# Attention in two passes over 16 head groups: the second pass starts 9 units behind the first, not 12

## The chip, the cores and the metric

The kernel runs on one core of one Trainium2 chip. The metric is the device time of one execution in microseconds. The kernel before took 2340.22 us, the median of three runs (2337.09 to 2341.55). The engines are named as the profile names them: PE is TensorE (matmuls and transposes), DVE is VectorE, ACT is ScalarE, POOL is GpSimd, and SP issues most of the DMAs. PSUM is the memory that PE writes its results to; a tile of it must be read out by DVE or ACT before PE can write there again.

## The reference

The input is four sequences of 1024 tokens with 256 features. The program is a layer stack: attention, a mixture of experts (4 experts, one per token), a Mamba2 block and the mixture again, each added to its input after a layernorm. The change lies in attention alone, which is, cut to what matters:

```python
ids = _adapter_ids(lora_start_indices, b)            # one low-rank adapter per sequence
Q = _multilora(x, ids, Wq, Aq, Bq)                   # K and V in the same way
Q, K, V = (split(Q), split(K), split(V))             # 16 heads of 16 features
Q, K = (_rope(Q), _rope(K))
scores = jnp.einsum('bhqd,bhkd->bhqk', Q, K) / jnp.sqrt(jnp.asarray(D_KV, x.dtype))
causal = jnp.tril(jnp.ones((s, s), bool))
scores = jnp.where(causal, scores, jnp.asarray(-jnp.inf, scores.dtype))
attn = jax.nn.softmax(scores, axis=-1)
out = jnp.einsum('bhqk,bhkd->bhqd', attn, V)
return _multilora(out, ids, Wo, Ao, Bo)
```

The softmax needs the maximum of each query's scores before the exponentials, and this is why the kernel computes the scores twice.

## The kernel before

**Groups and passes.** Attention treats 16 groups one after the other (`Heads`, numbered n): four sequences, and in each four groups of four heads. A group goes through three kinds of work.

- *Pieces* prepare its operands (`piece`, L833). `rotated` multiplies 256 tokens with the merged weights (qkv, L780), applies the rotary embedding on POOL, and `split` divides each query and key into a rounded value and a remainder, so that matmuls with rounded operands keep the precision. `turn` (L824) transposes 512 tokens of them with four PE transposes, and ACT casts the result to SBUF (L831).
- *The first pass* is 12 units (`first_pass`, L951): query block qb of 128 queries against keys 0 to 511 (h = 0) or 512 to 1023 (h = 1), as far as the causal mask allows. In `maxima` (from L848) each unit has two halves p of two heads: two score matmuls (L857) into a PSUM tile of two banks, a mask addition on DVE where the block touches the diagonal (L865), and a maximum on DVE (L866). The widths of the units in order are 128, 256, 384, 512, 512, 128, 512, 256, 512, 384, 512, 512; units 0, 1, 2, 3, 5, 7, 9 and 11 have the mask. `negated` (L868 to L885) turns the maxima of 512 queries around: a few small DVE operations into the tile mm, four PE transposes into a PSUM tile (L883), and a DVE copy to mneg (L885). It runs for queries 0 to 511 after unit 3 and for queries 512 to 1023 after the last unit.
- *The second pass* is also 12 units (`second_pass`, L952): query half qt of 512 queries against key block kc of 128 keys. Units 0 to 3 have qt = 0 with widths 512, 384, 256 and 128; units 4 to 11 have qt = 1 with 512 five times and then 384, 256, 128. Each half p recomputes the scores with keys on the partitions (L893), adds the negated maxima by a second pair of matmuls with mneg, takes the exponential on ACT (L901), and cuts the diagonal block on POOL (L904). `weigh` (L912) then multiplies with the values, in four column tiles of 32, into one accumulator bank, and `divide` sends the sums out and back to divide them. Units from 4 on need the mneg of the second half of the queries.

**Order.** `attention` is written as loops. In a prologue before the second pass of group 0, the list `beside` puts pieces of group 0 and group 1 next to the 12 first-pass units of group 0. Then the loop over n goes through the 12 units u of group n's second pass. Beside unit u stands unit u of the first pass of group n + 1 (through `look`), a piece of group n + 2, and steps of generators: `begin` starts the next sequence's layernorm and transposes, `finish` multiplies with the output weights and routes tokens to experts, and `tiles` are tiles of the first mixture of experts. `weigh` of a unit runs in the unit behind it. The two last turns of a group, those for tokens 512 to 1023 (pieces 12 and 13), come at units 0 and 1 of the next group's loop. A scheduler takes this program and sets the order of each engine's queue by its own plan, so that the queues differ from the written order where data allow it.

**PSUM.** In attention, PSUM is cut into three tiles of two banks for the scores of both passes (and for the experts), one tile of a single bank, and one bank for the accumulator. The single bank serves, one after another in program order, the turns, qkv, mneg, the transposes of the layernorm's output (xT), the output projection and the routing. In the prologue, turns and qkv use the two-bank tiles instead.

Of the kernel before, what the change touches and what calls it, by code (L numbers as in the profile page):

```python
# [78 lines left out]
def hybrid_block(ctx: ExitStack, tc: tile.TileContext, t, out: bass.AP):  # L79
# [81 lines left out]
    def layernorm(pool, xs, xln, name, pinned=False):  # L161
        n = xs.shape[1]
        stats = pool.tile([P, n, 6], F32, tag="ln_stats", name=f"stats_{name}", bufs=2)
        mv = pool.tile([P, n, 2], F32, tag="ln_mv", name=f"mv_{name}", bufs=2)
        rstd = pool.tile([P, n], F32, tag="ln_rstd", name=f"rstd_{name}", bufs=2)
        for i in range(n):
            first = nc.vector.bn_stats(stats[:, i, :], xs[:, i, :])
            if pinned and i == 0:
                tc.keep_in_program_order(first)
            nc.vector.bn_aggr(mv[:, i, :], stats[:, i, :])  # L170
        nc.vector.tensor_single_scalar(rstd, mv[:, :, 1], EPS, op=ALU.add)
        rsqrt(rstd, name)
        shift = pool.tile([P, n], F32, tag="ln_shift", name=f"shift_{name}", bufs=2)
        nc.vector.scalar_tensor_tensor(shift, mv[:, :, 0], -1.0, rstd, op0=ALU.mult, op1=ALU.mult)
        for i in range(n):
            nc.scalar.activation(
                xln[:, i, :], xs[:, i, :], AF.Identity, bias=shift[:, i : i + 1], scale=rstd[:, i : i + 1]
            )

    def transposed(xln, dst, name):  # L180

        for k in range(2):
            pt = ps1(f"xT_{name}_{k}")
            for i in range(4):
                nc.tensor.transpose(pt[:, i * P : (i + 1) * P], xln[:, i, k * P : (k + 1) * P], ident)
            evacuate(k, dst[:, k, :], pt)
# [430 lines left out]
    def attention(pa):  # L617
# [54 lines left out]
        def merge(b, weff):  # L672
            btm = pa.tile([LR, HG, 3, 64], F32, tag="btm", name=f"btm_{b}")
            nc.vector.tensor_scalar_mul(btm, bt_qkv, msk[:, b : b + 1])
            for k in range(2):
                pm = ps2(f"merge_{b}_{k}")
                for h in range(2):
                    for w in range(3):
                        nc.tensor.matmul(
                            pm[:, h, 0:384].rearrange("p (c w e) -> p c w e", c=2, w=3)[:, :, w, :],  # L680
                            a_qkv[:, w, k * P : (k + 1) * P],
                            btm[:, 2 * h : 2 * h + 2, w, :],
                            start=True,
                            stop=True,
                        )
                nc.vector.tensor_tensor(
                    weff[:, k, :].rearrange("p (h o) -> p h o", h=2),
                    pm[:, :, 0:384],
                    weff[:, k, :].rearrange("p (h o) -> p h o", h=2),
                    ALU.add,  # L690
                )
            return weff
# [16 lines left out]
        def begin(b):  # L709
            B = batches[b] = Batch()  # L710
            B.xT = pa.tile([P, 2, SEQ], F32, tag="xT", name=f"xT_{b}")
            B.o = [pa.tile([P, SEQ], F32, tag="o", name=f"o_{b}_{k}", bufs=3) for k in range(2)]
            for g in range(2):
                other = b == 0 and g == 1
                xln = pa.tile([P, 4, D], F32, tag="pe" if other else "x", name=f"x_{b}_{g}", bufs=4 if other else 1)
                nc.sync.dma_start(xln, t["x"][b, g * TB : (g + 1) * TB].rearrange("(n p) d -> p n d", p=P))
                if g == 0:
                    weff = pa.tile([P, 2, HG * 192], F32, tag="weff", name=f"weff_{b}")
                    nc.sync.dma_start(weff, t["w_qkv"].rearrange("(k p) o -> p k o", p=P))
                if b == 0:  # L720
                    yield
                layernorm(pa, xln, xln, f"a{b}_{g}")
                if g == 0:
                    B.weff = merge(b, weff)
                yield
                transposed(xln, B.xT[:, :, g * 512 : (g + 1) * 512], f"a{b}_{g}")
                yield
# [223 lines left out]
        first_pass = [(qb, h) for qb in range(NBLK) for h in range(qb // 4 + 1)]  # L951
# [3 lines left out]
        def look(H, u, p):  # L955
            qb, h = first_pass[u]
            H.maxima(qb, h, p)
            if p == 0:
                return
            if (qb, h) == (3, 0):  # L960
                H.negated(0)
            if u == len(first_pass) - 1:
                H.negated(1)


        first = begin(0)
        next(first)
        load_more()
# [3 lines left out]
        H, after = heads[0], heads[1]  # L972
# [4 lines left out]
        for which in range(2):  # L977
# [9 lines left out]
            lambda: after.project(2),  # L987
            lambda: [after.turn(0, 1, p) for p in range(2)],
            lambda: after.project(3),
            lambda: [after.turn(1, 0, p) for p in range(2)],  # L990
            lambda: [after.turn(1, 1, p) for p in range(2)],
            lambda: None,
        ]
        for u in range(len(first_pass)):
            beside[u]()
            for p in range(2):
                look(H, u, p)
# [29 lines left out]
        for n, H in enumerate(heads):  # L1027
            after = heads[n + 1] if n + 1 < len(heads) else None
            then = heads[n + 2] if n + 2 < len(heads) else None
            for u, (qt, kc) in enumerate(second_pass):  # L1030
                if after and n and u < 2:
                    after.piece(12 + u)

                pes = []
                for p in range(2):
                    off, pe = H.exps(qt, kc, p)
                    pes.append(pe)
                    if after:
                        look(after, u, p)
                    if p == 0:  # L1040
                        weigh_late()
                late = (H, qt, kc, off, pes)
                step()
                if then:
                    then.piece(u)
                if H.c == 0 and n and u == 6:
                    sending = finish(H.b - 1, 1)
                if H.c == HG - 1 and u == 10:
                    sending = finish(H.b, 0)
                if H.c == 1 and H.b + 1 < NB and u == 8:  # L1050
                    starting = begin(H.b + 1)
                next(starting, None)
                next(sending, None)
                if u not in (0, 1, 5, 6):
                    next(tiles, None)
                if H.c == 1 and n > 1 and u == 1:
                    for _ in tiles:
                        pass
                    tiles = stage(2 * H.b)
# [382 lines left out]
    for n, H in enumerate(halves):  # L1442
        after = halves[n + 1] if n + 1 < len(halves) else None
# [94 lines left out]
```

## Time and profile before

| what | value |
|---|---|
| median of three runs | 2340.22 us |
| the profiled execution | 2337.63 us |
| its span, first to last instruction | 2335.9 us |
| mean granted PE clock | 0.946 |
| PE busy in the span | 2121.0 us, 91% |
| DVE busy | 1375.6 us, 59% |
| ACT busy | 866.6 us, 37% |
| POOL busy | 844.7 us, 36% |
| maxima of the first pass on DVE (L866), 384 | 363.7 us |
| exponentials on ACT (L901), 384 | 308.8 us |
| weigh matmuls on PE (L912), 1536 | 263.5 us |
| first matmul of the second pass of group 0 | at 82.6 us |
| last matmul of the second pass of group 15 | at 1160.1 us |

The span is one execution. Busy time is a sum over an engine's instructions, with overlap counted once. The shares are averages over the whole program; the stage that the change touches is the first half. The clock is the share of full speed that the chip granted to PE.

### The profile page before, as it was taken

The page shows a single profiled execution, that of the slowest core. Times are in us where ns is not written, and L with a number is a line of the kernel's source. Part 1 is how long each engine was busy: PE and PEld are TensorE (multiplying, and loading weights), DVE is VectorE, ACT ScalarE, POOL GpSimd, SP SyncE. Part 2 cuts the span into 40 slices and gives each one's busy share as a digit, 9 for nine tenths or more (in the row PEclk, how much of TensorE's full clock was granted, in tenths as well). Part 3 has the DMA queues.
Part 4 walks back from the last instruction along what each step waited for, and adds up shares of the span by engine and source line. Part 5 has one row for each costly group of instructions (what it writes and reads, how often), then busy time and mean ns, then how long its engine had stood idle before and what let it go on. Part 6 is the DMA issues. An engine that isn't in the chain of part 4 may idle for free. (4 is left out here: it accounts for less than half of the span.)

```text
span 2335.9 us, 34795 instructions
## 1 busy us (share of the span) xinstructions
PE 2121.0 (91%) x12322; PEld 1484.7 (64%) x12322; DVE 1375.6 (59%) x3536; ACT 866.6 (37%) x1709; POOL 844.7 (36%) x1455
## 2 busy tenths in 40 slices
PE   5899998999999998999988986989899999999997
PEld 4444454554455555655677983557677777879887
DVE  5666666656655455655254336777777777676422
ACT  3365544455544443343310114444333333332110
POOL 3343434244443333321111213665535343343121
PEclk8799998999999999999999997899999999899999
DMA  9101011300132121132246780002435354344788
GB/s 332 33 28 42 22 35 56 104 24 20 44 127 84 59 83 60 41 126 81 95 153 231 252 284 27 1 28 70 159 109 192 108 188 147 131 160 149 272 301 305
DMA packets 148976, 278.19 MB, mean 119 GB/s; under 512 B 19964, under 2 KB 92030, under 8 KB 148800
## 3 DMA queue, kind: packets, MB, share of 16 engines
q1 hardware_dynamic: 120768, 227.98, 28.3%
q0 software_dynamic: 9920, 30.25, 3.5%
q10 hardware_dynamic: 18112, 17.70, 2.5%
q8 instruction: 100, 1.64, 0.3%
q14 instruction: 76, 0.62, 0.1%
HBM read 225.17 MB, written 51.12 MB: 118 GB/s over the span
## 5 line engine op out<-in xcount | busy, mean ns | idle before, releaser
L866 DVE TENSOR_REDUCE mx<-s 128x2 f32<-128x1024 f32 (+3 forms) x384 | 363.7, 953 | 82.8 <-PE s L857 76.6
L901 ACT ACTIVATE pe<-s 128x1024 f32<-128x1024 f32 (+3 forms) x384 | 308.8, 810 | 247.2 <-PE s L893 185.2
L912 PE MATMUL acc<-pe,v 128*32 128x512 f32 (+3 forms) x1536 | 263.5, 516 | 13.6 <-POOL pe L904 11.7
L904 POOL TENSOR_SCALAR_AFFINE_SELECT pe<-pe 128x256 f32<-128x256 f32 x256 | 103.9, 407 | 440.4 <-ACT pe L901 440.1
L469 PE MATMUL gu_f<-t_xT_f,t_Wg_f 128*128 128x128 f32 (+1 forms) x1216 | 239.8, 320 | 4.6 <-DVE t_xT_f L141 2.3
L469 PE MATMUL gu_f<-t_xT_f,t_Wu_f 128*128 128x128 f32 (+1 forms) x1216 | 235.3, 317 | 1.6 <-DMA t_Wu_f<-in_Wu 1.6
L469 PEld LDWEIGHTS gu_f<-t_xT_f,t_Wg_f 128*128 128x128 f32 x1216 | 186.8, 196 | 26.9 <-issue 7.1
L865 DVE TENSOR_TENSOR s<-s,amats 128x256 f32<-128x256 f32 x256 | 109.1, 428 | 153.9 <-PE s L857 113.8
L469 PEld LDWEIGHTS gu_f<-t_xT_f,t_Wu_f 128*128 128x128 f32 x1216 | 188.9, 196 | 13.3 <-DMA t_Wu_f<-in_Wu 2.4
L485 PE MATMUL y_f<-t_Wd_f,t_h_f 128*128 128x256 f32 x816 | 187.3, 383 | 7.4 <-DVE t_rows_f L492 2.7
L857 PE MATMUL s<-ks,qs 64*128 64x512 f32 (+3 forms) x768 | 171.8, 398 | 23.1 <-ACT pe L901 13.5
L893 PE MATMUL s<-qs,ks 64*128 64x512 f32 (+3 forms) x768 | 181.7, 439 | 10.1 <-DVE mx L866 7.6
L893 PEld LDWEIGHTS s<-qs,ks 64*128 64x128 f32 x768 | 79.5, 188 | 170.9 <-issue 96.3
L159 DVE SCALAR_TENSOR_TENSOR t_h_f<-t_h_f,gu_f 128x512 f32<-128x512 f32 x102 | 69.8, 684 | 195.5 <-ACT t_h_f L158 195.5
L485 PEld LDWEIGHTS y_f<-t_Wd_f,t_h_f 128*128 128x128 f32 x816 | 152.8, 191 | 38.0 <-issue 6.7
L158 ACT ACTIVATE t_h_f<-gu_f 128x512 f32<-128x512 f32 x102 | 60.8, 596 | 279.1 <-PE gu_f L469 279.1
L893 PE MATMUL s<-mneg,sel_r 64*128 64x512 f32 (+3 forms) x768 | 160.2, 364 | 0.0
L857 PEld LDWEIGHTS s<-ks,qs 64*128 64x128 f32 x768 | 84.3, 194 | 73.9 <-ACT pe L901 26.3
L1221 DVE SCALAR_TENSOR_TENSOR xc_m<-raw_m,conv_w,xc_m 128x512 f32<-128x512 f32 x144 | 112.3, 790 | 22.2 <-ACT xc_m L1217 15.8
L1171 POOL TENSOR_TENSOR m_m<-m_m,gm_m 128x256 f32<-128x256 f32 x128 | 94.2, 768 | 58.1 <-ACT gm_m L1314 57.0
L780 PE MATMUL qkv<-weff,xT 128*128 128x192 f32 x512 | 105.9, 352 | 8.2 <-ACT ks L831 4.6
L780 PEld LDWEIGHTS qkv<-weff,xT 128*128 128x128 f32 x512 | 86.2, 199 | 28.7 <-ACT ks L831 10.5
(448 smaller groups left out, 3935.0 us busy)
## 6 DMA issues: line engine op xcount, KB each, us to landing
t_Wg_f<-in_Wg SPq DMA_DIRECT2D x38, 1024.0 KB
t_Wu_f<-in_Wu SPq DMA_DIRECT2D x38, 1024.0 KB
t_Wd_f<-in_Wd SPq DMA_DIRECT2D x38, 1024.0 KB
sorted_rows<-blank SPq DMA_DIRECT2D x8, 2056.0 KB
t_Wg_f2p<-in_Wg SPq DMA_DIRECT2D x10, 1024.0 KB
t_Wu_f2p<-in_Wu SPq DMA_DIRECT2D x10, 1024.0 KB
t_Wd_f2p<-in_Wd SPq DMA_DIRECT2D x10, 1024.0 KB
t_Wg_f1p<-in_Wg SPq DMA_DIRECT2D x9, 1024.0 KB
```

The costliest lines, as they stand in the source:

```text
L469: nc.tensor.matmul(gu[:, i, j, :], w[which][:, k, f * P : (f + 1) * P], xT[:, k, :], start=(k == 0), stop=(k == 1))
L485: nc.tensor.matmul(y, hs[f // nf][:, f % nf, i * P : (i + 1) * P], wd[:, f, :], start=(f == 0), stop=(f == DFF // P - 1),)
L780: nc.tensor.matmul(pp[:, i, 0:192], B.xT[:, k, tok], B.weff[:, k, self.c * 192 : (self.c + 1) * 192], start=(k == 0), stop=(k == 1),)
L857: nc.tensor.matmul(sc[:, a, 0:w], self.q[p, qb // 4][r, qb % 4 * P : (qb % 4 + 1) * P], self.k[p, h][r, 0:w], start=True, stop=True,)
L865: nc.vector.tensor_tensor(sc[:, :, w - P : w], sc[:, :, w - P : w], bcast(amats, 1, 2), ALU.add)
L866: nc.vector.tensor_reduce(self.mx[:, qb, 2 * p : 2 * p + 2, h], sc[:, :, 0:w], axis=AX.X, op=ALU.max)
L893: nc.tensor.matmul(sc[:, a, off:512], sels[p][r, :] if part else self.k[p, kc // 4][r, kc % 4 * P : (kc % 4 + 1) * P], self.mneg[qt][r, of ...
L901: nc.scalar.activation(pe[:, :, off:512], sc[:, :, off:512], AF.Exp, scale=1.0 / math.sqrt(DK))
L904: nc.gpsimd.affine_select(diag, diag, [[0, 2], [1, P]], ALU.is_ge, 0.0, base=0, channel_multiplier=-1)
L912: nc.tensor.matmul(self.acc[32 * j : 32 * j + 32, off:512], self.v[:, kc, (DK + 1) * j : (DK + 1) * j + 32], pes[j // 2][:, j % 2, off:512 ...
L1171: nc.gpsimd.tensor_tensor(*operands(slice(i, i + size)), op)
L1221: nc.vector.scalar_tensor_tensor(acc, raw[:, k : k + TB], conv_w[:, cc, k : k + 1], acc, op0=ALU.mult, op1=ALU.add)
```

## The change

`LAG` is 9. The prologue computes only the first 9 first-pass units of group 0, and the three last entries of `beside` go: two of them were the four turns of group 1's tokens 512 to 1023, and the last was empty. These turns are now pieces 12 and 13 of the loop for group 0 too. In the loop, unit u of a group's second pass has beside it, for u = 0 to 2, the group's own first-pass units 9 to 11, and for u = 3 to 11 the first-pass units 0 to 8 of the next group. With this, `negated` for the first half of the queries falls at u = 6 of the group before (it was u = 3), and for the second half at u = 2 of the group itself (it was u = 11 of the group before). The last group, which had no first-pass unit beside it, now has its own three.

```diff
+        LAG = 9
+
         first = begin(0)
...
             lambda: after.project(3),
-            lambda: [after.turn(1, 0, p) for p in range(2)],
-            lambda: [after.turn(1, 1, p) for p in range(2)],
-            lambda: None,
         ]
-        for u in range(len(first_pass)):
+        for u in range(LAG):
             beside[u]()
             for p in range(2):
                 look(H, u, p)
...
             for u, (qt, kc) in enumerate(second_pass):
-                if after and n and u < 2:
+                if after and u < 2:
                     after.piece(12 + u)
 
                 pes = []
                 for p in range(2):
                     off, pe = H.exps(qt, kc, p)
                     pes.append(pe)
-                    if after:
-                        look(after, u, p)
+                    ahead = LAG + u
+                    if ahead < len(first_pass):
+                        look(H, ahead, p)
+                    elif after:
+                        look(after, ahead - len(first_pass), p)
                     if p == 0:
                         weigh_late()
```

The functions that are called (`piece`, `turn`, `maxima`, `negated`, `exps`, `weigh`) are the same in both kernels.

## Prediction

> **What bounds the kernel now.** I read first the slices of the span, to see which engine is full where the change acts (attention fills the first half, slices 1 to 20 of 58.4 us each).
>
> ```profile
> PE   5899998999999998999988986989899999999997
> ...
> DVE  5666666656655455655254336777777777676422
> ...
> PEclk8799998999999999999999997899999999899999
> ```
>
> TensorE is 90% busy or more from the third slice on, VectorE 50 to 60%. The exceptions are the first two slices. The table of busy time by stretches splits them (each row: stretch and length in us; then busy time of PE, its weight loads, DVE, ACT, POOL; granted clock; DMA share; GB/s):
>
> ```profile
> core 0: us, PE busy (x) PEld busy (x) DVE busy (x) ACT busy (x) POOL busy (x), PEclk, DMA share, GB/s
> ...
> 60.00:70.00 10.00, 7.37 (x38) 5.55 (x38) 5.74 (x10) 2.41 (x9) 4.08 (x8) 0.84 0.30 94
> 70.00:82.60 12.60, 9.68 (x34) 4.75 (x34) 7.37 (x10) 3.67 (x10) 4.09 (x8) 0.50 0.00 1
> 82.60:137.20 54.60, 51.56 (x290) 25.23 (x290) 36.96 (x76) 28.67 (x57) 22.25 (x47) 0.84 0.03 11
> 137.20:193.00 55.80, 51.70 (x346) 27.55 (x344) 35.28 (x59) 30.23 (x59) 23.98 (x49) 1.00 0.13 44
> ```
>
> 82.6 us is where the second pass of group 0 starts, 137.2 where that of group 1 starts (first L893 matmul of each). Before 82.6 no engine is full and the clock ends at half; from 82.6 on TensorE is busy 92 to 99% of every group. The loop over groups is bound by TensorE, and runs to the last L893 at 1160.1.
>
> The waits of TensorE between 82.6 and 1160.1, longest first, show what is left there:
>
> ```profile
> PE s L857 <- ACT pe L901: 13.5, 17, 1.8
> PE acc L912 <- POOL pe L904: 11.7, 11, 1.7
> PE s L893 <- DVE mx L866: 7.6, 13, 1.0
> PE qkv L780 <- ACT ks L831: 4.6, 9, 1.5
> PE mneg L883 <- ACT qk L792: 4.2, 2, 2.1
> ```
>
> All visible waits there are 72.5 us over 16 groups (my sum of the idle times over 100 ns), 2.5 to 8 us in each. By unit of the second pass they lie at units 0 (10.8), 3 and 4 (25.6), 11 (9.9). The last two rows are the single-bank PSUM tile: its next writer waits until ScalarE has emptied it.
>
> **The change, part by part.** Price list, from the trace at full clock: a first-pass unit costs TensorE 0.3 us per pair of 512-wide matmuls (two pairs a unit; 0.23 at 384) and VectorE 1.22, 0.95, 0.69 or 0.42 us per maximum by width plus 0.43 per mask; four transposes of turn 0.6 us plus a 0.58 us cast on ScalarE; qkv 1.5 us on TensorE; an exp 1.02 us; the mneg copy 0.69 us.
>
> *The start.* TensorE at the end of the prologue:
>
> ```profile
> 69.89 1.50 PE L857 MATMUL s<-ks,qs 64*128 64x512 f32 x4
> 71.31 1.17 PE L824 MATMUL turn<-mats,qtok 128*128 128x128 f32 x3
> 74.00 1.33 PE L824 MATMUL turn<-mats,qtok 128*128 128x128 f32 x5 [1.51 <-POOL qtok L816]
> 75.57 1.01 PE L857 MATMUL s<-ks,qs 64*128 64x384 f32 x4 [0.25 <-ACT qs L831]
> ...
> 79.35 2.91 PE L857 MATMUL s<-ks,qs 64*128 64x512 f32 x8
> 82.60 0.80 PE L893 MATMUL s<-qs,ks 64*128 64x512 f32 x2 [0.34 <-DVE mx L866]
> ```
>
> The first row is unit 8 (query block 6, keys 0 to 511), the ninth and last that the prologue keeps. What is dropped stands from 71.3 to 82.6: 11.2 us. Group 0's loop keeps twelve first-pass units (its own last three, nine of group 1), so only the four turns of group 1 are added to it: 4 x 0.6 = 2.4 us at full clock, 4.8 at half. Start of group 1: -11.2 + 2.4 = -8.8, or -6.4. VectorE owes the three units 2 x (0.95 + 0.43) + 2 x 1.22 + 2 x (1.22 + 0.43) = 8.5 us and some 2.5 for the maxima's negation by unit 4; group 0's units 0 to 3 took 23.4 us, so it keeps pace there. I take -7.5. At the other end the last group, 53.3 us long with TensorE busy 52.6, gets three units it had not: 2 x 0.23 + 4 x 0.3 = 1.7, with changes of tiling 2. **Ends: -5.5** (bounds -9 and -2).
>
> *The order of TensorE's instructions.* The same matmuls are issued; the built program stands in another order almost everywhere. Counting in both orders: the four column-tiled weigh matmuls of a tile stand in 285 runs instead of 287 (a 512-wide run costs 1.0 us however many of the four it holds; the runs saved are wide ones), worth -1.6; lone halves of L857 and L893 pairs -1.8; so -3.4. Against it: the tile configuration (128x128 for qkv, turn and FFN; 64x128 for scores; 128x32 for weigh) changes 1044 times against 1023. In the trace the step from qkv into L893 takes 255 ns where a step inside takes 163, from L469 into L893 309 against 216: 0.093 each. The Trainium skill, page "TensorEngine Tiling (Array Packing)", section "Key Properties", says that a change of tiling mode, unlike one of tile, drains TensorE. By the row with that rule the 21 more cost 2.0, so **-1.4**; with no such price it would be -3.4. I take -1.4.
>
> *VectorE beside TensorE, in all groups.* A group's work is the same; only which units stand together changes. Before, units 10 and 11 of the second pass (128 to 256 wide, little work for TensorE) stand beside first-pass units 10 and 11 (512 wide): VectorE owes 5.7 us there where TensorE has 4.0, and 1.9 more for the negation; this is the L893 <- mx wait at unit 0. After, they stand beside units 7 and 8: 4.7 against 3.8. Units 2 and 3 are 6.1 against 3.9 before, 6.4 against 4.3 after: no change. My walk through group 3 (51.0 us before) gives 18.2 for units 0 to 3 (18.7), 26.9 for 4 to 9 (27.1), 4.0 for 10 and 11 (5.0). Some ten groups are like it; but the exp and affine_select waits, the two largest rows, are not touched. Between +3 (nothing gained and a few new meetings) and -12 in all: I take **-5**, nearest to half of what unit 0's 10.8 us shows.
>
> *The negation of half 1 comes late.* This speaks against. It stood at unit 11 of the group before, five units ahead of its first use (unit 4, L893's second part); now it stands at unit 2, two units ahead. The PSUM tile it goes through is a single bank, handed on in program order: turn, turn, qkv (unit 0), turn, turn, qkv (unit 1), mneg. One link is matmul plus emptying: in group 2 of the trace turn follows turn after 1.33 us (208.61 to 209.94), qkv is followed after 2.5. The chain is 4 x 1.33 + 2 x 2.5 + 1.35 = 11.7 us, against 14 to 19 us of units 0 to 3: it fits in a plain group at no cost, as units 0 to 3 hide it. Its DVE ops (reduce, four on mm, one copy) are queued behind the maxima of unit 11, and L893's second part, behind which every later exp and weigh of the group waits, is the first to suffer. In **group 2** the cover is gone: the second layernorm half of batch 1 puts its transposes (xT) on the same bank, at 203.7 to 207.9 us in this trace. In the new order xT, turn, turn, qkv, turn, turn, qkv, mneg stand with two S matmuls between them: 1.3 + 11.7 = 13.0 us of links with 0.6 + 2.4 + 3.0 + 0.6 + 0.3 = 6.9 of TensorE in them, so 6 of stall, where before the same stretch (208 to 223) shows 1.5; and 1.6 more for an exp behind ScalarE's copies. The clock: this trace grants 0.50 for 3.4 us from 219.5, after this very 1.5 us wait. The Trainium skill, page "TensorE: Matmul & The Clock Gate", section "What's actually happening", gives the half clock only after an idle window of about 3.4 us; by that rule six short stalls cost no clock, by the row they bring another such stretch or two, 1.7 us each. I go by the row. So +4 to +8: **+5**. In **groups 5 and 9** VectorE has 8.3 us of the router's tables between the mm copies and the mneg copy: +1.5 to +2.5 each; in 4, 8 and 12 the emptying waits grow by some 1 together and shrink in 12. **+3** (bounds 0 and +8).
>
> *DMAs.* None moves against the second pass: the loads of x, the sums, dens and inv round trips, FFN weights on SP's queue hang on second-pass units, and come earlier with them by the start's gain. SP has nothing new ahead of it; POOL's rope operations for group 1 are unmoved, its other pieces stand at the same units. Nothing is charged.
>
> **Sum.** -5.5 - 1.4 - 5 + 5 + 3 = -3.9. Made against the profiled execution (2337.6; span 2335.9 and 1.7 around it): 2333.7. The median shown, 2340.2, is 2.6 above that execution, and the same sum from it is 2336.3; I forecast the middle, 2335.
>
> **Rivals.**
> 1. *Slower: the late negation decides.* The single-bank chain ends after unit 4's S matmuls are due in more groups than 2, as each meets exps and casts on ScalarE (a link of 2 in place of 1.33 makes the chain 16 to 18 us, which units 0 to 3 no longer hide). With 1.5 us lost in each of 15 groups beyond what is summed: -3.9 + 22 = +18; with half of it +7. It decides once it takes over 4 us plus the 4.7 that a measurement can tell, 0.6 us a group. For it: qkv and mneg waits on ScalarE are already 8.8 us, and units 3 and 4 the worst. Against: plain groups have 3 to 7 us of slack by the trace. About 2350.
> 2. *Larger gain:* VectorE's backlog at units 10 to 0 vanishes in all groups and its stalls at unit 11 and 0 (20.7) halve, with the ends at -9: some -18, 2322. Against: the largest part of these waits is on ScalarE and POOL.
> 3. *Nothing:* what the start gains lies in a prologue bound by chains of rope and casts on POOL and ScalarE, and comes back as waits of group 0, since its qkv and turns for group 1 are as late as before (qtok at 74.0 came from POOL). The loop then starts its units early and waits: 2340.
>
> **How the numbers follow.** 0.2% of 2340 is 4.7 us, about what a measurement of this kernel can tell from no change: faster is below 2335.5, slower above 2344.9. The sum's own case has 0.40, its own range 2328 to 2342, of which 0.25 counts as faster and 0.15 as within; rival 2 0.18; rival 3 0.07; rival 1 0.35. So faster 0.43, same 0.22, slower 0.35. Adding all lower ends gives about -18 (2320), all upper ends about +15 and rival 1 beyond them: I take 2319 to 2352.
>
> **What would show it.** First L893 near 71 to 73 us and that of group 1 near 130: the start. Group 15 at 55 us. Group 2 longer by about 5, with mneg or qkv waiting on ScalarE at its units 3 and 4; if such waits appear in groups 1, 3, 7 too, rival 1 is right. L893 <- mx at unit 0 smaller: the VectorE step. Group 3 at 49 to 51 us says whether plain groups gain. Wrong would be: group 1 starting at 137 as before, or plain groups above 52.

## The result, and the profile after

The changed kernel took 2354.02 us, the median of 20 runs (2343.05 to 2364.79). The kernel before took 2338.66 us, the median of 20 runs beside them. The ratio is 1.0068, with a 95% interval of 1.0052 to 1.0084: slower by 12 to 20 us. The forecast was 2335.

The profiled execution took 2362.74 us (span 2361.0, mean clock 0.926). Over the 20 runs the clock had a median of 0.9335, so this is one of the longer ones, and its excess of 25 us over the profiled execution of before is more than that of the medians.

The slices of the changed kernel:

```profile
PE   5898999999999999999988996888899999999997
...
DVE  5555666566655445656344335787767767675522
...
PEclk8787999898889999999999997889899999999999
```

PE is as full as before, 9 in nearly every slice of attention. The clock is not: of slices 3 to 20 it shows 7 or 8 in six, where before it was one. The table of stretches (columns as before) starts with the first L893 at 72.0 us; the rows are the groups 0, 1, 2 and 3:

```profile
72.00:133.70 61.70, 55.78 (x308) 28.64 (x304) 36.20 (x76) 31.77 (x65) 26.07 (x56) 0.83 0.03 10
133.70:190.20 56.50, 53.66 (x343) 28.95 (x342) 34.67 (x58) 29.98 (x59) 23.77 (x49) 0.88 0.13 42
190.20:259.00 68.80, 60.07 (x326) 30.55 (x326) 37.35 (x86) 32.55 (x64) 24.40 (x50) 0.80 0.08 25
259.00:312.90 53.90, 50.74 (x323) 26.71 (x322) 33.88 (x57) 29.64 (x58) 24.16 (x50) 0.91 0.07 21
```

The loop starts 10.6 us earlier, but group 1 only 3.5 us earlier. Group 2 takes 68.8 us (56.4 before). Group 3 takes 53.9 (51.0), with PE busy 3.4 us longer at a clock of 0.91. Groups 2 and 3 of the kernel before, in the same view:

```profile
193.00:249.50 56.50, 52.16 (x323) 26.19 (x322) 37.05 (x86) 31.87 (x63) 24.20 (x50) 0.97 0.10 29
249.50:300.40 50.90, 47.38 (x317) 24.55 (x316) 32.48 (x57) 29.67 (x58) 23.97 (x49) 1.00 0.08 23
```

The waits of PE in the loop, the same view as before:

```profile
PE s L857 <- ACT pe L901: 15.6, 30, 1.5
PE s L893 <- ACT pe L901: 10.6, 12, 2.1
PE acc L912 <- POOL pe L904: 8.2, 11, 1.6
PE mneg L883 <- DVE mm L880: 5.8, 7, 1.8
PE qkv L780 <- ACT qs L831: 4.2, 3, 2.1
```

L893 on the maxima, 7.6 us before, has nearly gone; waits on ScalarE's exponentials and on mm have taken its place. The sum of waits over 100 ns is 72.3 us, against 72.5.

**A ledger of the loop.** I split the length of the loop, first to last L893, into four parts. Waits are PE's gaps over 100 ns, and shorter gaps stand for themselves. For the rest, each form of matmul has a mean duration at full and at half clock, over all traces (a 512-wide L893 with q and k 219 and 357 ns). Time at half clock is then cut into what the same instruction takes at full clock, called work, and the remainder, called clock loss.

| loop | length | work | clock loss | waits | short gaps | half-clock time |
|---|---|---|---|---|---|---|
| before | 1077.5 | 968.5 | 35.2 | 72.2 | 1.7 | 86 |
| changed | 1120.0 | 968.7 | 77.2 | 72.3 | 1.9 | 191 |
| changed, a second execution | 1119.0 | 969.7 | 71.9 | 75.4 | 2.1 | 179 |

Of the 42.5 us by which the loop grew, 42.0 are clock loss. Work and waits are equal. The second execution is that of run e14 below. Both executions of the changed kernel are long ones (the second is the longest of its 13), so that the medians, 15 us apart, hold a smaller part of this loss. Groups 1, 3 and 7, called plain below, had no clock loss before; they have 5.5, 3.8 and 5.6 us of it in the first execution, 5.6, 4.2 and none in the second. After attention the profiled execution of before was slower than this one (1175.8 against 1169.0 us from the last L893 to the end of the span; the other kernels below lie between 1162 and 1172), which hides part of it.

The times without a profile say the same. Each run lists its mean clock. In 20 runs of the changed kernel time falls by 13.4 us for each 0.01 of clock (correlation -0.93), in 92 runs of the kernel before by 15.7 (-0.81). At a clock of 0.940 the fitted lines give 2344.9 us for the changed kernel and 2345.7 for the one before. The kernel before has a median clock of 0.947, the changed one 0.9335.

### The profile page after: what moved, and what is told of

Same layout as the page of the kernel before. It is cut to its first block, busy times and chain, and to the rows that moved or that the text cites. A ratio compares the mean times of both kernels' runs of the same rounds, so it can differ in the third digit from the quotient of the medians.

```text
span 2361.0 us, 34842 instructions
## 1 busy us (share of the span) xinstructions
PE 2153.7 (91%) x12322; PEld 1505.5 (64%) x12322; DVE 1377.0 (58%) x3536; ACT 866.0 (37%) x1709; POOL 840.9 (36%) x1455
## 5 line engine op out<-in xcount | busy, mean ns | idle before, releaser
L893 PEld LDWEIGHTS s<-qs,ks 64*128 64x128 f32 x768 | 83.1, 195 | 193.4 <-issue 115.4
L893 PE MATMUL s<-qs,ks 64*128 64x512 f32 (+3 forms) x768 | 193.3, 462 | 12.5 <-ACT pe L901 10.6
L857 PE MATMUL s<-ks,qs 64*128 64x512 f32 (+3 forms) x768 | 171.6, 403 | 22.8 <-ACT pe L901 15.6
L893 PE MATMUL s<-mneg,sel_r 64*128 64x512 f32 (+3 forms) x768 | 162.2, 384 | 1.3 <-DVE mneg L885 1.3
L857 PEld LDWEIGHTS s<-ks,qs 64*128 64x128 f32 x768 | 86.5, 202 | 72.5 <-ACT pe L901 34.0
L795 POOL TENSOR_TENSOR rope<-qk,rope 128x256 f32<-128x256 f32 x62 | 45.2, 729 | 224.0 <-ACT qk L792 223.8
L1223 DVE SCALAR_TENSOR_TENSOR xc_m<-raw_m,conv_w,xc_m 128x512 f32<-128x512 f32 x144 | 111.8, 786 | 21.8 <-ACT xc_m L1219 15.1
L780 PE MATMUL qkv<-weff,xT 128*128 128x192 f32 x512 | 114.3, 372 | 8.9 <-ACT qs L831 4.2
L780 PEld LDWEIGHTS qkv<-weff,xT 128*128 128x128 f32 x512 | 94.3, 214 | 35.5 <-ACT qs L831 11.5
```

Source lines behind the costliest of these rows:

```text
L780: nc.tensor.matmul(pp[:, i, 0:192], B.xT[:, k, tok], B.weff[:, k, self.c * 192 : (self.c + 1) * 192], start=(k == 0), stop=(k == 1),)
L857: nc.tensor.matmul(sc[:, a, 0:w], self.q[p, qb // 4][r, qb % 4 * P : (qb % 4 + 1) * P], self.k[p, h][r, 0:w], start=True, stop=True,)
L893: nc.tensor.matmul(sc[:, a, off:512], sels[p][r, :] if part else self.k[p, kc // 4][r, kc % 4 * P : (kc % 4 + 1) * P], self.mneg[qt][r, of ...
L1223: nc.vector.scalar_tensor_tensor(acc, raw[:, k : k + TB], conv_w[:, cc, k : k + 1], acc, op0=ALU.mult, op1=ALU.add)
```

## The experiments

The theories when the first runs were made: A, the loss is half clock that follows gathered waits; B, it is the waits or the order themselves; C, exponentials stand on ScalarE behind casts that wait for GpSimd; D, the negation of the second half is late because of the order on the single PSUM bank (rival 1). "Late" is measured as the distance, in unit 4, from the first L893 matmul to the first with mneg:

```
group                   0    1    2    3    4    5    6    7    8    9   10   11   12   13   14   15
before                0.6  0.2  0.3  0.2  0.2  0.3  0.2  0.2  0.2  0.3  0.2  0.2  0.3  0.2  0.3  0.3
changed               3.9  1.5 21.9  1.5  3.8  8.2  4.5  1.5  4.7  8.2  7.0  6.6  0.3  0.3  6.1  6.2
third experiment      0.6  0.5  1.7  0.5  0.6  0.3  0.3  0.5  0.6  0.3  0.3  0.3  0.3  0.3  0.3  0.3
```

This distance is not yet a wait, and the bank is not its reason everywhere. The transposes of mneg need two things: the tile mm, which VectorE makes from the maxima, and an empty bank. In both executions of the changed kernel the bank is the last of the two in groups 2, 5 and 9, by 19.0, 9.1 and 9.1 us, and in groups 4 and 8 by 0.3 us. In the nine other late groups it had been empty for 4 to 12 us when mm was ready. And in groups 4, 6, 8, 10, 11, 14 and 15 PE does 16 matmuls of the router or of the experts between the two parts of unit 4, work that it owes in any case. (The experts' outputs, y at L483, pass through the single bank too; the list of its users ahead of the prediction leaves them out.)

**e1: matmuls that nobody reads, at unit 3 of the changed kernel.**

```diff
+                if (qt, kc) == (0, 3):
+                    for _ in range(4):
+                        for a in range(2):
+                            r = slice(64 * a, 64 * a + 64)
+                            nc.tensor.matmul(sc[:, a, 0:off], self.k[p, 0][r, 0:P], self.q[p, 0][r, 0:off],
+                                             start=True, stop=True)
```

> The changed kernel with work added: after the score matmuls of unit 3 of each second pass (128 columns wide) eight more pairs of score matmuls write the unused 384 columns of the same PSUM tile; nobody reads them. They cost TensorE 16 groups x 8 x 0.23 = 29 us if nothing hides them, and they stand where the plain groups wait 1.2 and 0.9 us. Theory A (the loss is the half clock that follows a cluster of waits at unit 3): the drops at unit 3 of groups 1, 3 and 7 go, half-clock time in the attention loop falls from 191 us toward 120, and the added work is paid back: 2340 to 2354. Theory B (the loss is the waits themselves, or the order; the clock only follows): the waits stay or are filled without gain, and the time is 2360 to 2383.

2354.33 us, ratio to before 1.008 (1.0046 to 1.0113): as slow as the changed kernel, with up to 29 us more to do. Half-clock time fell from 191 to 140 us. In groups 1, 3 and 7 it fell from 38 to 14 us together, and they became shorter by 3.7, 2.7 and 2.4 us although each had eight pairs more. Group 3 in this run:

```profile
248.20:299.40 51.20, 48.58 (x339) 27.31 (x338) 34.12 (x57) 29.43 (x58) 24.25 (x50) 0.97 0.07 22
```

By the ledger the work and the waits of each of these groups stayed within 0.6 us, and their clock loss fell from 14.9 to 4.9 us together, so it speaks for A in these groups. The drops did not go, as A had it: each group still has 3.4 to 6.8 us at half clock. Over the loop work rose by 9 us and waits by 13, as much as the clock loss fell (22), and the total at A's upper edge doesn't decide. The fill changed the planner's order too: the weigh matmuls stand in 265 uninterrupted stretches (284 in the changed kernel), and mneg is late in groups 2, 5 and 9 alone. So in 11 groups the lateness went and the time did not.

**e2: the rounding casts on GpSimd.**

```diff
-                        nc.scalar.copy(wn[:, n].bitcast(F32R), bcast(r[:, n], 2, 2))
+                        by.tensor_copy(wn[:, n].bitcast(F32R), bcast(r[:, n], 2, 2))
```

> The changed kernel, but the rounding casts of split (16 a group) are made by GpSimd, which makes the rotation before them and the remainder after them, instead of ScalarE. Theory C (the wait at unit 3 is an exponential that stands on ScalarE behind casts that wait for GpSimd's rotation: 2.6 us at 272.9 in group 3): the 1.22 us wait of L857 on L901 goes in groups 1, 3 and 7, with it the drop of the clock, 2336 to 2347; GpSimd gets about 0.15 us more per cast. Theory D (the single PSUM bank: mneg of the second half waits for turn, turn, qkv, turn, turn, qkv): no change, 2350 to 2358.

2368.58 us, ratio 1.0141 (1.0103 to 1.0178). Waits of L857 on exponentials fell from 15.6 to 7.2 us, as C says, but waits of weigh on GpSimd's diagonal cut rose from 8.2 to 31.1 us: GpSimd then had too much ahead of it. C's mechanism is seen, and its gain was not to be had in this way.

**e3: mneg of the second half through a two-bank tile.**

```diff
-                pt = ps1(f"mneg_{self.name}_{qt}")
+                pt = one_of_two(f"mneg_{self.name}_{qt}") if qt else ps1(f"mneg_{self.name}_{qt}")
```

> The changed kernel, but the transposes of the negated maxima of the second half go through a two-bank score tile, not the single bank, so that they no longer queue behind the turns and qkv. Theory D (the order on the single bank makes mneg late): group 2 falls from 69 to 60 us or less, the mneg waits at unit 4 go, 2338 to 2347. Theory C (exponentials behind casts): the wait of 1.22 us at unit 3 of groups 1, 3 and 7 stays, 2348 to 2358, also because a score tile is taken for a while.

2330.81 us, ratio 0.9969 (0.9951 to 0.9987): 23 us less than the changed kernel, and faster than the kernel before. The lateness is gone in all groups (table above), as D says. D's numbers were not met: group 2 fell to 64.1 us, not 60, and the time is 7 us below D's range. Group 2 in the changed kernel, and then in this one (a PE timeline: start, length, line, the wait ahead of it and what ended it):

```profile
212.51 0.66 PE L824 MATMUL turn<-mats,qtok 128*128 128x128 f32 x4
...
213.84 1.10 PE L824 MATMUL turn<-mats,qtok 128*128 128x128 f32 x4 [0.26 <-ACT qs L831]
215.61 2.93 PE L780 MATMUL qkv<-weff,xT 128*128 128x192 f32 x8 [0.68 <-ACT qs L831]
219.17 1.12 PE L824 MATMUL turn<-mats,ktok 128*128 128x128 f32 x4 [0.63 <-ACT qk L792]
220.96 1.12 PE L824 MATMUL turn<-mats,ktok 128*128 128x128 f32 x4 [0.68 <-ACT ks L831]
223.12 2.93 PE L780 MATMUL qkv<-weff,xT 128*128 128x192 f32 x8 [1.04 <-ACT ks L831]
226.68 1.12 PE L883 MATMUL mneg<-mats,mm 128*128 128x128 f32 x4 [0.63 <-ACT qk L792]
228.58 1.22 PE L893 MATMUL s<-mneg,sel_r 64*128 64x512 f32 x4 [0.78 <-DVE mneg L885]
```

```profile
197.83 0.52 PE L883 MATMUL mneg<-mats,mm 128*128 128x128 f32 x3 [1.80 <-DVE mm L880]
...
203.32 1.12 PE L824 MATMUL turn<-mats,qtok 128*128 128x128 f32 x4
...
204.37 1.21 PE L893 MATMUL s<-mneg,sel_r 64*128 64x512 f32 x2
```

In the first, mneg is the seventh link of the chain on one bank, each link waits for ScalarE's emptying, and from the second turn on it runs at half clock (a turn 1.12 in place of 0.66 us, qkv 2.93 in place of 1.57). It starts 36 us into the group. In the second it starts 14 us into the group, ahead of the turns. The ledger of e3: work 948.6, clock loss 55.9, waits 79.6. Against the changed kernel work is 20 lower and clock loss 21; waits are 7 higher. The lower work I had not expected. The weigh matmuls of the loop stand in 260 uninterrupted stretches, 284 in the changed kernel: fewer quadruples are cut apart by other matmuls. In the traces at full clock a run of 512-wide weigh matmuls takes 0.98 us with one of the four in it and 1.00 with all four (0.76 and 0.78 at 384 columns, 0.55 and 0.57 at 256, 0.34 and 0.36 at 128). So a cut costs 0.3 to 1.0 us by width, and 24 cuts less are most of the 20.

So the gain can't be put down to the queue on the bank. Groups 2, 5 and 9, the ones that the bank held up, gave 4.2 of the 34 us by which the loop became shorter. The lower work is a matter of order (e5 has it too), and clock loss is still 21 us above that of the kernel before, with mneg in time everywhere.

**e4: the pieces moved by three units too.** Pieces 9 to 13 of a group then come at units 0 to 4 of the next loop.

```diff
-                if after and u < 2:
-                    after.piece(12 + u)
+                late_piece = 12 + u - 3
+                if after and late_piece < 14 and (n or late_piece >= 12):
+                    after.piece(late_piece)
...
-                if then:
-                    then.piece(u)
+                if then and u >= 3:
+                    then.piece(u - 3)
```

> The changed kernel with the pieces of the group after next (qkv, rotation, split, turns) moved by the same three units as the first pass, from unit u to unit u + 3, so that they stand beside the same first-pass units as in the kernel before. Then units 0 to 2 hold no qkv and no casts, and mneg of the second half has only two turns ahead on its bank. Theories C and D both say that the waits at units 2 to 4 go: half-clock time well under 191 us, 2325 to 2345. If the loss lay in the narrow score units standing beside narrow first-pass units at unit 3, whatever the pieces do, the drops at unit 3 stay or move to unit 6, where qkv now stands: 2350 to 2365.

2401.42 us, ratio 1.027 (1.0231 to 1.0309): a miss for all of them. Work is 998.7, in 320 weigh stretches (36 more than the changed kernel, 30 us more work), waits 92.5, clock loss 65.7. The new place cut the weigh matmuls, which none of the theories had in it. In the plain groups mneg is 3.0 us late although the bank was empty 12 to 14 us before mm was ready, which speaks against D there.

**e5: the edit of e3 on the kernel before.**

> The kernel before with the one edit of the third experiment: the transposes of the negated maxima of the second half go through a two-bank score tile. In the kernel before they start 3 us into the group and are needed 16 to 25 us into it, so Theory D (the bank's order costs only where it makes mneg late) expects no gain: 2333 to 2345, a score tile being taken for 1.4 us more per group. If the edit helps by itself, whatever the lag (fewer writers on the single bank), it gains here what it gained there, about 23 us: 2310 to 2320.

2355.95 us, ratio 1.0078 (1.0047 to 1.0108). No gain, as D says, but slower than D's range. The edit lowers the work here too, by 24 us to 944.0, although no mneg was late; clock loss (54.5) and waits (77.7) rose against that, and the loop began at 89.2 us in place of 82.6. So the lower work of e3 is not lateness undone, and clock loss can rise by 19 us without lateness. Its profiled execution, 2339.67, is its fastest; why its other runs are longer I did not find.

**e6, e7, e8: other lags.** `LAG` is 11, 10, and 10 with the edit of e3.

```diff
-        LAG = 9
+        LAG = 11
...
-            beside[u]()
+            if u < len(beside):
+                beside[u]()
```

> The changed kernel with LAG = 11, single bank as it was. The negation of the second half falls at unit 0, behind two turns on the bank and ahead of the first qkv; it is needed four units on. Theory D: the second part of unit 4 follows its first by under 1 us in all groups, as in the kernel before; half-clock time in attention near 80 to 140 us; 2328 to 2345. If any stand beside of a group's own last unit costs (the mask and maximum of 512 columns at unit 0, the turns of group 1 in the loop), it is as slow as LAG = 9: 2350 to 2358.

> The changed kernel with LAG = 10: the negation falls at unit 1, behind turn, turn, qkv, turn, turn on the bank and ahead of the second qkv; it is needed three units on. Theory D: between LAG = 9 and LAG = 11, the second part of unit 4 late by 0 to 3 us in plain groups, 2336 to 2350. If the order on the bank is not what matters but that unit 3 is narrow in both passes, LAG = 10 moves the wider unit 1 to unit 3 and should win all back: 2325 to 2337.

> LAG = 10 with the negation of the second half through a score tile. Theory D: as the third experiment, which has mneg in time, or better by its one more unit of slack: 2322 to 2336. If the score tile that the negation takes is what limits now, no better than LAG = 9 with it: 2330 to 2340.

2346.39 us, ratio 1.0043 (1.0027 to 1.0059), at 11; 2377.37, ratio 1.017 (1.0132 to 1.0207), at 10; 2355.21, ratio 1.0095 (1.0064 to 1.0126), at 10 with the edit. At 11 mneg is late in groups 2 (10.6 us), 10 (4.0), 5 and 9 (2.1) and 11 (1.0), where D had expected none, and the loss is some 60% of that at 9, 1 us above D's range. At 10 plain groups are in time (0.2 us), but groups 2, 5 and 9 are late by 19.9, 12.8 and 10.9 and six others by 3 to 4, and group 5 alone takes 103.8 us (84.8 before); the time is beyond both expectations. So the loss is not ordered by lag. With the negation on the bank, the bank ends last in groups 2, 5 and 9 at each of the three shorter lags, by 9 to 20 us. With mneg off the bank, LAG = 10 wins 22 us, about what LAG = 9 does, but lies 18 us above the kernel before with mneg in time in every group (work 977.8, clock loss 61.0), beyond both expectations too.

**e9: the four turns back in the prologue, LAG = 9.**

```diff
-            lambda: after.project(3),
+            lambda: (after.project(3), [after.turn(1, w, p) for w in range(2) for p in range(2)]),
...
-                if after and u < 2:
+                if after and n and u < 2:
```

> The changed kernel with one of its parts undone: the four turns of group 1 (tokens 512 to 1023) go back into the prologue, beside its ninth unit; the loop's pieces 12 and 13 start with n = 1 again. Theory D: only group 0 changes; its loop starts 2 to 5 us later and loses 2.4 us of work, and everything from group 1 on stands as in the changed kernel: 2350 to 2359. If the moved turns are a main cause of the loss (they open group 0's chain on the bank), 2337 to 2347.

2341.33 us, ratio 1.0026 (1.0007 to 1.0044): 12.7 us less than the changed kernel (10 by the two ratios, as the kernel before was 3 us faster beside this run), a miss for D's number and in the range for the turns as a main cause. Group 0 shows where:

```profile
79.30:125.40 46.10, 43.57 (x280) 20.09 (x278) 36.74 (x76) 27.36 (x51) 19.02 (x41) 0.94 0.04 13
```

The loop starts 7.3 us later than in the changed kernel (79.3), but group 1 starts 8.3 us earlier (125.4 against 133.7), at a clock of 0.94 in place of 0.83. By the ledger group 0 has 6.3 us less work, 5.9 less clock loss and 3.5 less waits. The bank is not the reason: in the changed kernel it was empty at 90.4 us and mm ready at 96.4, so mneg did not wait for the turns. From group 1 on most groups are within 1.3 us of the changed kernel; 7, 8 and 10 are shorter by 3 to 5 us at a higher clock.

**e10, e11, e12: variants of e3.** e10 is LAG = 11 (e6) with the edit of e3. The edits of e11 and e12 to e3 are these, the second with the loop body of e1 three times:

```diff
-                pt = one_of_two(f"mneg_{self.name}_{qt}") if qt else ps1(f"mneg_{self.name}_{qt}")
+                pt = one_of_two(f"mneg_{self.name}_{qt}")
```

```diff
+                if (qt, kc) in ((0, 2), (0, 3)) and p == 1:
+                    for _ in range(3):
```

> LAG = 11 with the negation of the second half through a score tile. It has four units of slack and no queue. In the built program the weigh matmuls stand in 264 stretches (286 in the kernel before, 261 in the third experiment, one more costs about 0.8 us by the experiments so far). If the stretches and the clock are the whole account: 2336.8 - 18 at the clock of the kernel before (0.946) = 2319, up to 2336 at a clock of 0.935. If lateness on the bank were all, LAG = 11 has little of it and the edit brings nothing on its 2346: 2340 to 2350.

> LAG = 9 with both negations through score tiles. 256 stretches, five fewer than the third experiment, 4 us; the negation of the first half (unit 6 of the group before) is not late in any run so far, so nothing else is expected: 2318 to 2334. If a score tile taken longer costs more than that, 2334 to 2345.

> The third experiment with score matmuls added that nobody reads: three pairs after the second half of units 2 and 3 (256 and 384 columns), 16 x 3 x (0.15 + 0.23) = 18 us of work if nothing hides it. Theory A (the clock falls where waits gather in the narrow units): drops at units 2 to 4 of groups 1, 3 and 7 go, the median clock rises from 0.940 and the work is paid back: 2318 to 2334. Without such an effect it costs its 18 us: 2340 to 2350.

2362.26 us (1.0116, 1.0072 to 1.016), 2337.67 (1.0023, 0.9998 to 1.0047) and 2356.07 (1.0079, 1.0052 to 1.0107). e10 has mneg in time everywhere and the low work that its 264 stretches promised (949.9), and loses it to waits (92.7) and clock (68.7): counting stretches does not forecast a time, and neither range was met. e11 has 255 stretches and more waits (87.7), no better than e3. e12 tests A where mneg is not late, and is slower than expected even without A's effect: clock loss fell by 3 us at most, while work rose by about 15 and waits by 17. Keeping TensorE busy with idle matmuls is no remedy here.

**e13, e14, e15: the two parts apart.** e13 is the kernel before with the turns alone moved; e14 is the changed kernel once more; e15 is e3 with e9's edit. The edit of e13 to the kernel before:

```diff
-            lambda: [after.turn(1, 0, p) for p in range(2)],
-            lambda: [after.turn(1, 1, p) for p in range(2)],
+            lambda: None,
+            lambda: None,
...
-                if after and n and u < 2:
+                if after and u < 2:
```

> The kernel before (LAG of 12) with one part of the change done alone: the four turns of group 1 for tokens 512 to 1023 leave the prologue and become pieces 12 and 13 of group 0's loop. If moving them costs about 8 us or more by itself (the ninth experiment took back 12.7 us by undoing it): 2343 to 2352. If it costs only beside the shorter lag, where the negation of group 0 stands behind these turns on the single bank: 2332 to 2340.

> The changed kernel itself once more, on the chip of the next and the previous run, since the ninth experiment was timed on another chip: 2349 to 2359 if chips do not matter. Its trace shows how much the half-clock stretches of one and the same program differ between two executions: the loop's half-clock time was 191 us in the first one, at a clock of 0.926; at the median clock of 0.9335 it should be 150 to 165.

> The two edits that helped together: LAG = 9, the negation of the second half through a score tile (third experiment, 6 us faster than the kernel before), and the four turns back in the prologue (ninth, 12.7 us faster than the changed kernel). If they add up: 2315 to 2322. If the ninth helped only because mneg of group 0 no longer queued behind its turns on the bank, which the third cures as well: 2326 to 2334. 262 stretches of weigh matmuls.

e13: 2332.54 us, ratio 0.9981 (0.9967 to 0.9996): moving the turns costs nothing at a lag of 12. e14: 2351.82 us, ratio 1.0071 (1.005 to 1.0092), the first measurement again; its profiled execution is once more a long one (2365.20), with 179 us at half clock, so the half-clock time of an execution near the median was not seen. e15: 2328.25 us, ratio 0.9951 (0.9935 to 0.9967), the fastest of all, 0.5% below the kernel before. e9's and e3's gains do not add (12.7 and 23 would give 2318): the loop of e15 starts 8.3 us later than that of e3 and is 8.7 us shorter, so that both end at 1157 us. The time is in the range that was expected if e9 had freed mneg of group 0 from the queue on the bank, but that is not why: in group 0 mneg had not waited for the bank (see e9).

Taken together, lateness does not order the times. In the kernel before, e13, e3, e15, e11, e8, e5 and e10 mneg is never more than 1.7 us late, and they took 2328 to 2362 us.

e14 also gives group 7 of one program in two executions, the changed kernel's first and second:

```profile
526.50:581.30 54.80, 52.54 (x323) 27.55 (x322) 33.86 (x57) 29.65 (x58) 24.22 (x50) 0.88 0.07 21
```

```profile
531.40:581.50 50.10, 47.23 (x323) 25.19 (x322) 33.55 (x57) 29.46 (x58) 24.16 (x50) 1.00 0.08 23
```

The group with its 323 matmuls takes 4.7 us more where the wait at unit 3 is followed by half clock. At full clock it takes 50.1 us, 0.9 less than in the kernel before.

## Why the prediction was wrong

**The step that failed** is "The negation of half 1 comes late", by its price: +5 for group 2, +3 for the others, and in a plain group "no cost". What the runs showed in its place is half clock, which the prediction charged in group 2 alone, as another stretch or two of 1.7 us. The loop lost 77.2 us to it in place of 35.2, which is all of its growth, and some 15 us of that (10 in the second execution) lie in the plain groups, which had none before.

The chain that the prediction walked was right for a plain group. In group 3 the bank was empty 11.3 us after the group's start (at 270.3), so the queue did fit. What came late was the other input: VectorE finished mm 17.2 us after the start, 1.1 us before unit 4 began. The prediction names these operations, queued behind the maxima of unit 11, and puts nothing on them.

**Rival 1** (forecast 0.35) has the sign, and its time, 2350, is 4 us from the median. That is in part luck. The second part of unit 4 was late in every group but 12 and 13, not in group 2 alone; but the chain on the bank, which is rival 1's reason, ended clearly last in groups 2, 5 and 9 only, and the stalls that it priced, 1.5 us in each of 15 groups, did not come.

**The price was of the wrong kind.** Prediction and rival 1 priced lateness almost wholly as stall. In the ledger the stalls did not grow at all (72.2 and 72.3 us), since other waits fell. What grew was the time at half clock, by 105 us in the profiled execution. Group 3 of the changed kernel shows a way in:

```profile
272.26 0.29 PE L893 MATMUL s<-mneg,sel_r 64*128 64x128 f32 x2
273.77 0.33 PE L857 MATMUL s<-ks,qs 64*128 64x128 f32 x2 [1.22 <-ACT pe L901]
...
276.29 1.12 PE L883 MATMUL mneg<-mats,mm 128*128 128x128 f32 x4 [0.93 <-DVE mm L880]
```

ScalarE in the same group, where a copy empties the bank and the exponential of unit 2 stands behind a cast, and the last operation for mm on VectorE:

```profile
269.96 0.38 ACT L792 COPY qk<-qkv 128x256 f32<-128x256 f32 x1
272.93 0.30 ACT L813 CAST qtok<-rope 128x128 fp32r<-128x128 f32 x1 [2.59 <-POOL rope L803]
273.13 0.59 ACT L901 ACTIVATE pe<-s 128x512 f32<-128x512 f32 x1
...
275.75 0.48 DVE L880 TENSOR_TENSOR mm<-neg,mm 128x8 f32<-128x8 f32 x2
```

The cast waits 2.59 us for GpSimd's rotation and holds the exponential; that holds a score tile, so PE waits 1.22 us; the first pass's scores come late to VectorE, and its operations for mneg, queued behind them, make PE wait 0.93 us more. The two waits fall at unit 3, where both passes have 128 columns and PE has little else. Then the clock is at half for 10.2 us. In the kernel before, mneg of this group started 15.8 us ahead of its use, which leaves room for a delay of this size:

```profile
252.61 0.66 PE L883 MATMUL mneg<-mats,mm 128*128 128x128 f32 x4 [0.29 <-DVE mm L880]
...
268.40 0.40 PE L893 MATMUL s<-mneg,sel_r 64*128 64x512 f32 x2
```

**The other steps.**
- *The start*: the first L893 was forecast near 71 to 73 us and came at 72.0. The moved turns were put at 2.4 to 4.8 us; by e9 they delay group 1 by 8.3 us, in work, clock and waits of group 0, and not through the bank. -7.5 was -3.5. At the other end group 15 took 56.3 us, 3.0 more (forecast 2).
- *The order of PE's instructions*: the loop's work is 0.2 us higher, with 1.7 of first-pass units and 2.4 of turns brought in from the prologue, so the order gave about -4 (-3 in the second execution), where -1.4 was taken and -3.4 was the sum without a price for changes of tiling. Right in sign, and too small to tell the two apart.
- *VectorE beside TensorE*: the wait of L893 on the maxima went, as forecast. At full clock a plain group takes 50.1 us for 51.0, about the 0.5 a group that was summed. It was lost again in the executions and groups where the clock fell: groups 1, 3 and 7 took 0.6, 2.9 and 3.7 us more.
- *Group 2*: longer by 12.4 us, not 5: 8.3 of clock loss and 4.4 of waits. Here mneg does wait for the bank, as forecast; with mneg off the bank (e3) the group is still 7.7 us longer than before. The links were taken at 1.33 and 2.5 us, their lengths at full clock; at half clock they were 1.8 and 3.6. *Groups 5 and 9*, forecast 1.5 to 2.5 us longer each, were 1.6 and 2.6 us shorter, although mneg was 8.2 us late in both.
- *Rivals 2 and 3*: the maxima's wait did vanish, but without gain in the sum of waits; the start was given back only in part.
- *Two readings of the profile* were too high: of the slices of attention, 7 and 19 show 8, not 9, and PE is busy 89 to 98% of a group, not 92 to 99%. Nothing in the sum rests on them.

**What stays open.** Why the clock was lower is not settled. The bank does not explain it even where it holds mneg up: groups 2, 5 and 9 together lost 26.6 us to the clock in the changed kernel (25.7 in the second execution), 16.2 before and 15.1 in e3, but 15.1 in e2 too, where mneg is as late in them as in the changed kernel.

The granted clock changes at multiples of 3.41 us; a cut of the loop into such windows shows what half clock follows. Over all 17 traces, 115 of 120 windows at full clock with PE busy less than 50% were followed by half clock, 115 of 215 between 50 and 66%, and 44 of 4261 at 75% or more. So between 50 and 66% it went either way, and there the two kernels differ: below 66% the kernel before has 19 windows, and 9 of them are followed by half clock; the changed kernel has 17, and 16 are (12 of 15 in its second execution). The window with the waits at unit 3 has PE busy 64% in group 7 of both executions of the changed kernel; one was followed by half clock, the other not. In the kernel before, groups 3 and 7 have a window of 64% each, and neither was. What else decides, or how much of the difference is chance, these runs don't show.

## What to carry to other kernels

When a step is moved closer to its user, walk the queue of every buffer that it passes through, at the durations of a throttled engine, and walk the step's inputs as well: here the bank was clearly the last to come in three groups of 16, and mm, made from the maxima, in ten. An edit that helps need not help for the reason that it was made for: taking mneg off the shared bank was worth 23 us at a lag of 9, and most of that in groups that the bank had not held up. The shorter lag with that edit, and the turns left in the prologue, is 0.5% faster than the kernel before. Equal sums of waits don't mean equal times when the engine's clock differs; so compare clock and half-clock time group by group before explaining a difference by waits. In a program whose order a planner sets, a small edit can move the whole by 1% and more for other reasons (e4, e5, e7, e10), so an edit must be tried and not argued.

## What the runs showed of the hardware

- Half clock follows windows of 3.41 us in which PE was busy too little, and not only idle ones: in the changed kernel 16 of 20 drops follow a window with PE busy 39 to 64%, 13 of them 56 to 64%; no window of its loop is idle and no wait is longer than 2.4 us. It often lasts past windows that are full: of 38 windows at half clock with PE busy 95% or more, 17 were followed by another at half, and stretches reached 20.5 us. The Trainium skill, page "TensorE: Matmul & The Clock Gate", section "What's actually happening", has one idle window before half clock and one busy window before full; these traces show both changes less simply.
- Half clock does not double every matmul: a 512-wide L893 with q and k went from 219 to 357 ns (1.63), a run of the four column tiles of 512 from 1.00 to 1.86 us (1.87), 128-wide transposes from 153 to 281 ns (1.84).
- The four column tiles of a weigh matmul run side by side: one alone took 0.98 us at 512 columns, four together 1.00, so cutting a quadruple apart costs nearly a whole run (0.34 us at 128 columns).
